# LayerNorm as two matrix products, wide matmuls as two column tiles, and a new plan of the order

## The chip, the cores and the metric

The program runs on one core of one Trainium2 chip. Five engines work side by side, each through its own queue in order: TensorE (PE; PEld is its loading of weights), VectorE (DVE), ScalarE (ACT), GpSimd (POOL) and SyncE (SP, which here only starts DMAs). The metric is the device time of one execution in microseconds, the median of several runs. All data is float32.

## The reference

Eight batches of 256 tokens of width 128 go through one cross attention with a gate, and then through a stack of six layers. Cut to what matters:

```python
x = x + tanh(g_xattn) * xattn(layernorm(x), ctx, ctx, ...)   # 16 heads of 8, 256 x 256 scores
y = layernorm(x)
for i in range(6):
    y = attn_layer(shift_tokens(y), Wqkv[i], q_scale[i], k_scale[i], Wo[i]) + y
    y = ffn_layer(shift_tokens(y), ln_g[i], ln_b[i], W1[i], b1[i], W2[i], b2[i]) + y
x = x + tanh(g_ffn) * y

def attn_layer(x, Wqkv, qs, ksc, Wo):          # 16 heads of 64, inner width 1024
    q, k, v = split(x @ Wqkv)
    q, k = rotary(l2norm(q) * qs), rotary(l2norm(k) * ksc)
    return local_attention(q, k, v) @ Wo       # windows of 32, each sees itself and the one before

def ffn_layer(x, g, bln, W1, b1, W2, b2):
    mu = x.mean(-1); var = ((x - mu) ** 2).mean(-1)
    xn = (x - mu) / sqrt(var + 1e-5) * g + bln
    a, gate = split(xn @ W1 + b1)              # 341 columns each
    return a * gelu(gate) @ W2 + b2
```

`shift_tokens` moves the second half of the features one token on. The part that is rewritten is `xn` in `ffn_layer`.

## The kernel before

The stream of a batch lives transposed in SBUF (`st[b]`, features on the partitions, 256 tokens along the row, the shifted half stored one column on), so a slice of it is the stationary operand of a projection. A piece of work for one layer and one batch is called a sequence here; there are 6 x 8 = 48, numbered k = 8 l + b. Each sequence has: eight projections of q and k, 128 tokens x 512 columns (`project`, L555); squares on ACT, rotation on DVE and its sum on POOL (`square` L563, `rotate` L571, `rotate_add` L586); norms and their inverses; POOL's multiplication by them (`normalize`, L609); transposes of q and k (`qk_transpose`, L619) and their evacuation by ACT (`qk_evacuate`, L627); v in four spans (`v_project`, L634), already written as two products of 64 columns of weights each, which go to the two halves of the partitions; scores in tiles of 64 rows and 32 columns (`scores`, L653); softmax over DVE, POOL and ACT (L664 to L691); transposes of the probabilities (`p_transpose`, L698); attention (`attend`, L730); the output projection in two halves of four accumulating products (`o_project`, L748); its addition to the stream (`o_add`, L539 and L540).

Then comes the feed-forward part. `f_transpose` (L761) turns the stream back to tokens on partitions, as two transposes into a PSUM tile px. `f_stats` takes mean and variance of each token on DVE (bn_stats L203, bn_aggr L204) and adds eps on ACT (L206). `f_rstd` raises to the power -0.5 on POOL (L210). `f_norm` subtracts and multiplies on DVE (L214), into xn in SBUF. `f_back` (L777) transposes xn again, and `f_affine` (L782) applies ln_g and ln_b on ACT, since features are then on the partitions. `f_up` (L797) makes three products for the gate and three for the values, the third of each with 85 columns of weights; `f_gelu` (L804), `f_gate` (L810), `f_down` (L821) and `f_add` follow.

The cross attention of the eight batches (`cross`, pieces whose names begin with x) fills the first 200 us nearly alone and runs beside the first sequences.

PSUM has three pools of two buffers: `ps_p` (one bank: projections, v, px, most of the cross part), `ps_s` (two banks: scores, transposes, attend, the up products) and `ps_m` (one bank: output projection, the transposed xn, two of the three value products, down). A piece that needs a buffer waits until the last reader of the buffer's old tile is done. Where DVE and ACT both read one PSUM tile, they read one after the other.

The order is written out by hand, in a table. `PLAN` gives each piece a time in slots, a sequence comes 5 slots after the one before it, and `CROSS_SHIFT` moves the cross part of each batch. All pieces are sorted by that time and emitted in that order, and each engine's queue holds its own in the same order:

```python
    def at(k, piece, fn, *args):
        time = PLAN[piece]
        pieces.append((k * SLOTS + time, len(pieces), fn, args))
```

So several sequences overlap. In the steady part, the order on PE over one sequence's time is: down (fdo) of k, proj31 of k+4, fba of k+1, proj30 of k+4, sc00 and sc01 of k+3, gate products (fga) of k+1, pt1 of k+2, proj00 of k+5, value products (fva) of k+1, vp3, sc10, sc11, vp1, vp2 of k+3, attend of k+2, proj01 and proj10 of k+5, wo0 of k+2, proj11, pqt3 and pqt0 of k+4, wo1, proj21, vp0, pqt2, pqt1, then ftr of k+2, proj20, pt0. Piece names: ftr, fst, frs, fno, fba, faf are f_transpose to f_affine in that order; vp and ve are v and its evacuation; sq, rot, radd, ss, nrm, qe, pqt are square to qk_transpose above; ma, mx, sub, ex, rs, div are the softmax's steps; pt and pe the transposes of probabilities and their evacuation; oe the evacuation of attend.

Weights of a layer are loaded by SP (`load_layer`, L475 to L500) into pools of two buffers, as soon as the last reader of the layer before the last is done.

Of the kernel before, what the change touches and what calls it, by code (L numbers as in the profile page):

```python
# [17 lines left out]
P = 128  # L18
# [12 lines left out]
FCH = [(0, 128), (128, 128), (256, FF - 256)]  # L31
EPS = 1e-5
# [5 lines left out]
    "clr": -73.7292947, "scb": -70.0069797, "ld0": -35.0162171, "ld1": -12.5813247,  # L38
    "tab": -7.6683787, "proj00": 2.0661479, "rot00": 2.4025502, "sq00": 2.5554862,
    "proj01": 3.2529434, "rot01": 3.3214336, "proj10": 3.5071971, "sq01": 3.6104712,  # L40
    "proj11": 3.6885065, "rot10": 3.7356190, "ss0": 3.7720268, "sq10": 3.7886707,
    "rot11": 3.8350533, "sq11": 3.8724995, "ss1": 3.9918618, "proj21": 4.0448072,
    "sq21": 4.3781883, "radd1": 4.3924623, "rot21": 4.4758648, "proj20": 4.8425580,
    "rot20": 5.5697729, "sq20": 5.5713267, "radd0": 5.9042720, "proj31": 6.2244486,
    "ss2": 6.2710763, "sq31": 6.3406736, "proj30": 6.4849253, "rot31": 6.5498143,
    "sq30": 6.6199673, "rot30": 6.7542538, "radd2": 6.9297661, "ss3": 7.1340866,
    "radd3": 7.2930704, "norms": 7.3485381, "ninv": 7.5627076, "nrm0": 7.5645782,
    "nrm3": 7.6018457, "nrm1": 8.2038284, "nrm2": 8.5657430, "pqt3": 8.6901898, "qe30": 8.8084477,
    "pqt0": 8.8257991, "vp0": 9.0734647, "qe31": 9.2292320, "pqt2": 9.2331941, "qe00": 9.3130114,
    "qe01": 9.3703632, "ve0": 9.3828160, "pqt1": 9.4414715, "qe21": 9.4630469, "qe10": 9.5406248,  # L50
    "qe20": 9.6465658, "qe11": 9.6687562, "sc00": 11.4869562, "sc01": 11.5828198,
    "ma0": 11.6476475, "mx0": 11.7176783, "vp3": 12.3428719, "sc10": 12.3554151,
    "ve3": 12.3847098, "sc11": 12.5047342, "sub0": 12.5264914, "ex0": 12.6176090,
    "vp1": 12.6566462, "vp2": 12.7494513, "ma1": 12.7820149, "ve2": 12.8886442, "rs0": 12.9868968,
    "ve1": 13.0757847, "mx1": 13.8703536, "div0": 14.6942876, "pt0": 14.9561638,
    "sub1": 15.0941710, "pe00": 15.1903495, "ex1": 15.7662187, "pe02": 15.9880113,
    "rs1": 16.3923268, "pe01": 16.6012453, "div1": 16.6632054, "pt1": 16.8318843,
    "pe12": 16.9812383, "pe10": 17.0871542, "pe11": 17.1065885, "at00": 17.8598296,
    "at01": 18.1229096, "at10": 18.2090149, "at11": 18.2185563, "oe0": 18.3505974,
    "wo0": 18.6691075, "oe1": 18.7595325, "wo1": 18.8332231, "oadd": 19.4264539,  # L60
    "ftr": 19.5952591, "fst": 19.8667684, "frs": 20.2036030, "fno": 20.9271736, "fba": 21.2395826,
    "faf": 21.7154140, "fga": 21.7794201, "fge": 21.8634391, "fva": 22.1636116, "fgt": 22.7262591,
    "fdo": 25.8686930, "fad": 27.9976703, "ldn": 28.7587942, "zt": 45.0036545, "zg": 45.1826346,
    "xld": -30.5179940, "xst": -28.7483611, "xrs": -28.2094646, "xno": -28.0294722,
    "xt": -25.8919641, "xte": -25.0068817, "xqk": -24.7151093, "xqe": -24.3960041,
    "xke0": -24.1822220, "xke1": -23.5897625, "xvp": -19.0992115, "xs1": -18.8011010,
    "xm11": -18.7695610, "xm12": -18.6001009, "xs0": -18.3761821, "xm10": -18.2076043,
    "xve": -18.1237548, "xm02": -18.0698775, "xm01": -18.0275400, "xs3": -17.5398786,
    "xm00": -17.3912921, "xm31": -17.3567125, "xm32": -17.2670533, "xm30": -16.6512482,
    "xs2": -16.4574966, "xm20": -15.6590289, "xm21": -15.4966539, "xb": -15.2142077,  # L70
    "xm22": -15.0420951, "xnt": -14.8243647, "xnc1": -14.7619952, "xp1": -14.7176089,
    "xnc2": -14.7060645, "xnc3": -14.7056110, "xe11": -14.6791462, "xe12": -14.6766048,
    "xe10": -14.4655074, "xnc0": -14.4380100, "xp0": -14.4183134, "xa1": -14.2088572,
    "xe02": -13.8510992, "xe01": -13.6172258, "xo1": -13.6088919, "xe00": -13.5855076,
    "xp3": -13.4284936, "xa0": -13.3512163, "xe31": -13.3313625, "xe32": -13.3038361,
    "xo0": -13.2546436, "xe30": -13.1766209, "xp2": -12.8009007, "xa3": -12.6439522,
    "xe22": -12.3901756, "xe21": -12.2805457, "xo3": -12.1606156, "xe20": -11.0882968,
    "xa2": -10.5369546, "xo2": -10.5038915, "xu1": -9.9444150, "xd1": -9.7892678,
    "xu0": -9.2798463, "xd0": -8.5766695, "xw": -7.7897065, "xc": -7.7481286, "xwo": -6.8890118,
    "xx": -6.8061458, "xst2": -6.6550961, "xr2": -6.5917848, "xn2": -6.4798693, "xt2": -5.6284344,  # L80
    "xsp": -5.5775580,
# [3 lines left out]
    -31.1859779, -28.1496673, -25.2253671, -22.2780463,  # L85
    -19.2671839, -16.3307478, -13.4009654, -10.5435620,
# [5 lines left out]
def tile_gated_block(ctx: ExitStack, tc: tile.TileContext, a: dict, out: bass.AP):  # L92
# [22 lines left out]
    def at(k, piece, fn, *args):  # L115
        time = PLAN[piece]
        pieces.append((k * SLOTS + time, len(pieces), fn, args))

# [12 lines left out]
    make_identity(nc, ident)  # L131
    half_neg = const.tile([P, 4], F32, name="half_neg")
# [86 lines left out]
    def cross(b):  # L219
# [32 lines left out]
        def x_project():  # L252
            pm = c_["pqk"] = ps_p.tile([P, 2, T], F32, tag="pj", name="pqk")
            for i in range(2):
                nc.tensor.matmul(pm[:, i, :], x_w[:, i, :], x_mid[:, i, :], start=True, stop=True)
# [15 lines left out]
        def x_values():  # L271
            pm = c_["pv"] = ps_p.tile([P, NT, D], F32, tag="pj", name="pv")
            for t in range(NT):
                nc.tensor.matmul(
                    pm[:, t, :], x_mid[:, 1, t * P : (t + 1) * P], x_w[:, 2, :],
                    start=True, stop=True,
                )
# [119 lines left out]
        def x_out():  # L397
            pm = c_["pout"] = ps_p.tile([P, NT, D], F32, tag="pj", name="pout")
            oT = c_.pop("oT")
            for t in range(NT):  # L400
                nc.tensor.matmul(pm[:, t, :], oT[:, t, :], x_w[:, 3, :], start=True, stop=True)
# [24 lines left out]
        kx = b + CROSS_SHIFT[b] / SLOTS  # L426
        for n, fn in (
# [8 lines left out]
            at(kx, n, fn)  # L436
        for part in range(2):
            at(kx, f"xke{part}", x_keys, part)
        for u in range(4):
            at(kx, f"xs{u}", x_scores, u)  # L440
            at(kx, f"xnc{u}", x_max_add, u)
            at(kx, f"xp{u}", x_scores_t, u)
            for x in range(3):
                at(kx, f"xm{u}{x}", x_maxima, u, x)
                at(kx, f"xe{u}{x}", x_exponentials, u, x)
            at(kx, f"xa{u}", x_attend, u)
            at(kx, f"xo{u}", x_attended, u)
        for t in range(NT):
            at(kx, f"xu{t}", x_turn, t)
            at(kx, f"xd{t}", x_divide, t)  # L450
# [20 lines left out]
    def load_layer(l):  # L471
# [14 lines left out]
        w["1"] = wpool.tile([P, 2 * FF], F32, tag="w1", name="w_1")  # L486
        nc.sync.dma_start(w["1"], a["L0_ffn_W1"][l])
# [56 lines left out]
    def sequence(k, l, b, weights):  # L544
# [4 lines left out]
        def project(c, half):  # L549
# [5 lines left out]
            nc.tensor.matmul(  # L555
# [188 lines left out]
        def o_project(half):  # L744
            first = "pwo" not in c_
            pm = once(c_, "pwo", ps_m, [P, T], "m")
            for c in range(4 * half, 4 * half + 4):
                nc.tensor.matmul(  # L748
# [8 lines left out]
        def f_transpose():  # L757
            px = ps_p.tile([P, NT, P], F32, tag="pj", name="px")
            c_["px"] = px
            for t in range(NT):  # L760
                nc.tensor.transpose(px[:, t, :], st[b][:, t * P : (t + 1) * P], ident)  # L761

        def f_stats():
            c_["mv"], c_["rstd"] = stats_of(c_["px"])
# [4 lines left out]
        def f_norm():  # L769
            c_["xn"] = wk.tile([P, NT, D], F32, tag="xn", name="xn", bufs=1)  # L770
            normalized(c_["xn"], c_.pop("px"), c_.pop("mv"), c_.pop("rstd"))

        def f_back():
            px = ps_m.tile([P, NT, P], F32, tag="m", name="pxt")
            c_["pxt"] = px
            for t in range(NT):
                nc.tensor.transpose(px[:, t, :], c_["xn"][:, t, :], ident)  # L777

        def f_affine():
# [3 lines left out]
                xnT, c_.pop("pxt").rearrange("p n t -> p (n t)"), AF.Identity,  # L783
# [3 lines left out]
        def f_up(s):  # L787
# [8 lines left out]
            for c, (o, m) in enumerate(FCH):  # L796
                nc.tensor.matmul(  # L797
                    dst[c][:m], w[:, s * FF + o : s * FF + o + m], c_["xnT"],
                    start=True, stop=True,
# [15 lines left out]
        def f_down():  # L815
            pm = ps_m.tile([P, T], F32, tag="m", name="pw2")
            c_["pw2"] = pm
            for c, (o, m) in enumerate(FCH):

                m += c == 2  # L820
                nc.tensor.matmul(  # L821
# [5 lines left out]

        for c in range(4):
            for half in range(2):
                at(k, f"proj{c}{half}", project, c, half)  # L830
                at(k, f"sq{c}{half}", square, c, half)
                at(k, f"rot{c}{half}", rotate, c, half)
                at(k, f"qe{c}{half}", qk_evacuate, c, half)
            at(k, f"pqt{c}", qk_transpose, c)
            at(k, f"ss{c}", squares_sum, c)
# [154 lines left out]
```

## Time and profile before

| | us |
|---|---|
| median of 3 runs | 1675.97 (1674.86 to 1676.92) |
| the profiled execution | 1670.12 |
| its span, first to last instruction | 1668.3 |
| PE busy in the span | 1601.3 |
| DVE, ACT, POOL busy | 1390.5, 1243.0, 1254.2 |
| start of the first projection of sequence 0 | 203.4 |
| first product of the output projection, sequences 10 and 11 | 593.4 and 622.3 |
| the same, sequences 46 and 47 | 1629.0 and 1645.4 |

A line of a timeline gives the start of a group of like instructions, the time from the first's start to the last's end, the engine, the source line, the operation, out <- in, the tile shape on the array (rows * columns), the shapes and the count. A float32 product shows as two records, a transpose as one. The ends of PE's records are modelled and overlap the next, so times on PE are taken between starts. Busy windows give, for each engine, the busy us in a stretch and the number of instructions; PEclk is the granted clock. The list of waits says who waited for whom, how long in total, and how often.

### The profile page before, as it was taken

What the parts mean: (1) busy time and instruction counts of PE and PEld (TensorE: products, weight loads), DVE (VectorE), ACT (ScalarE), POOL (GpSimd) and SP (SyncE); (2) the same over time, 40 slices, a digit from 0 to 9 for tenths busy, and PEclk for the clock granted to TensorE, in tenths of its full rate; (3) what the DMA queues carried; (4) which work ended last, traced back from release to release, by engine and by line L of the source; (5) the groups of instructions that cost most, each with busy time, mean ns of one, the idle gap of its engine ahead of it and who ended that gap; (6) DMA issues with size and microseconds to landing.
All of it is one profiled execution on the core that took longest, in us unless ns stands there. A gap on an engine that the chain in (4) does not pass through costs nothing.

```text
span 1668.3 us, 62716 instructions
## 1 busy us (share of the span) xinstructions
PE 1601.3 (96%) x28212; PEld 1011.2 (61%) x28212; DVE 1390.5 (83%) x1956; ACT 1243.0 (75%) x2084; POOL 1254.2 (75%) x714
## 2 busy tenths in 40 slices
PE   6989878999999999999999999999999999999996
PEld 3555534566666666666666666666666666666665
DVE  3455687899899989999899999899899999989964
ACT  3445447788787878888787888878787888878783
POOL 1112147988888898888888888888888988888871
PEclk8888899999999999999999999999999999999999
DMA  1300001000010000000000100000110000000000
GB/s 29 81 14 8 7 1 52 24 3 3 3 41 23 15 3 2 27 29 24 2 3 3 40 24 14 3 2 3 43 33 3 3 3 3 2 3 3 3 6 23
DMA packets 35208, 25.34 MB, mean 15 GB/s; under 512 B 16634, under 2 KB 31870, under 8 KB 34942
## 3 DMA queue, kind: packets, MB, share of 16 engines
q1 hardware_dynamic: 33646, 21.20, 4.4%
q8 instruction: 222, 3.64, 0.9%
q14 instruction: 44, 0.36, 0.1%
q10 hardware_dynamic: 1296, 0.14, 0.1%
HBM read 20.28 MB, written 1.05 MB: 13 GB/s over the span
## 4 chain that ended last, share of the span: by engine, by line
PE 86%; DVE 8%; ACT 3%; issue 1%; POOL 1%; DMA 1%; POOLq 0%; DVEq 0%; ACTq 0%
PE pj L555 21%; PE pv L634 11%; PE m L748 10%; PE s L653 8%; PE s L730 7%; PE pqt L619 6%; PE s L797 5%; PE pw L821 4%; DVE x_max L319 4%; PE ppt L698 4%; PE pa L797 2%; PE pssT L341 2%; PE pox L358 2%; ACT pr L351 1%; PE pssx L309 1%
## 5 line engine op out<-in xcount | busy, mean ns | idle before, releaser
L586 POOL TENSOR_TENSOR u<-ur 128x1024 f32<-128x1024 f32 x192 | 454.1, 2366 | 125.2 <-DVE ur L571 122.0
L555 PE MATMUL pj<-w_qkv,st 128*128 128x512 f32 x768 | 404.5, 619 | 9.0 <-ACT sq L563 2.8
L563 ACT ACTIVATE sq<-pj 128x512 f32<-128x512 f32 x384 | 229.5, 598 | 197.1 <-DVE ur L571 117.3
L609 POOL TENSOR_TENSOR u<-u,rn 128x1024 f32<-128x1024 f32 x192 | 359.2, 1900 | 3.6 <-DVE rn L602 3.6
L571 DVE TENSOR_TENSOR ur<-pj,rotk 128x1024 f32<-128x1024 f32 x192 | 234.7, 1222 | 63.9 <-PE pj L555 46.0
L571 DVE TENSOR_TENSOR ur<-pj,rotq 128x1024 f32<-128x1024 f32 x192 | 231.0, 1204 | 4.8 <-ACT sq L563 3.5
L580 DVE TENSOR_REDUCE squares<-sq 128x16 f32<-128x1024 f32 x192 | 232.1, 1209 | 0.9 <-ACT sq L563 0.7
L691 POOL TENSOR_TENSOR pr<-pr,rs 128x1024 f32<-128x1024 f32 x96 | 182.8, 1904 | 62.9 <-DVE rs L686 61.5
L210 POOL TENSOR_TENSOR rstd<-rstd,half_neg 128x2 f32<-128x2 f32 x64 | 45.0, 703 | 203.2 <-ACT rstd L206 187.2
L634 PE MATMUL pv<-w_qkv,st 128*64 128x512 f32 x768 | 197.1, 613 | 0.0
L748 PE MATMUL m<-oT,w_o 128*128 128x256 f32 x768 | 186.1, 386 | 0.0
L677 POOL TENSOR_TENSOR pr<-pr,top 128x1024 f32<-128x1024 f32 x96 | 182.7, 1903 | 1.1 <-DVE top L672 1.0
L653 PEld LDWEIGHTS s<-kT,qT 64*32 64x32 f32 x12288 | 127.2, 105 | 75.4 <-issue 40.3
L555 PEld LDWEIGHTS pj<-w_qkv,st 128*128 128x128 f32 x768 | 126.5, 190 | 72.6 <-issue 23.2
L748 PEld LDWEIGHTS m<-oT,w_o 128*128 128x128 f32 x768 | 141.9, 190 | 39.8 <-issue 21.5
L619 PEld LDWEIGHTS pqt<-ident,u 64*128 64x128 f32 x3072 | 102.9, 138 | 75.2 <-issue 39.7
L730 PEld LDWEIGHTS s<-prT,v 64*64 64x64 f32 x6144 | 122.0, 133 | 38.6 <-DVE hid L810 36.9
L653 PE MATMUL s<-kT,qT 64*32 64x64 f32 x12288 | 142.9, 225 | 0.0
L685 DVE TENSOR_REDUCE rs<-pr 128x16 f32<-128x1024 f32 x96 | 116.6, 1215 | 18.4 <-ACT pr L681 18.4
L319 DVE TENSOR_REDUCE x_max<-pssx 128x2 f32<-128x512 f32 (+1 forms) x96 | 77.5, 860 | 63.7 <-PE pssx L309 63.7
L730 PE MATMUL s<-prT,v 64*64 64x96 f32 (+1 forms) x6144 | 128.7, 238 | 0.0
L715 ACT ACTIVATE prT<-ppt,parity 128x256 f32<-128x256 f32 x192 | 121.4, 634 | 2.0 <-PE ppt L698 2.0
(112 smaller groups left out, 2674.9 us busy)
## 6 DMA issues: line engine op xcount, KB each, us to landing
w_qkv<-in_L_ffn_Wqkv SPq DMA_DIRECT2D x18, 512.0 KB
w_o<-in_L_ffn_Wo SPq DMA_DIRECT2D x24, 128.0 KB
w<-in_L_ffn_W SPq DMA_DIRECT2D x6, 341.0 KB
xin<-in_x SPq DMA_DIRECT2D x8, 128.0 KB
cin<-in_ctx SPq DMA_DIRECT2D x8, 128.0 KB
out<-res SPq DMA_DIRECT2D x8, 128.0 KB
w<-in_L_ffn_W SPq DMA_DIRECT2D x12, 64.0 KB
rotq<-in_c_cos_q SPq DMA_DIRECT2D x6, 64.0 KB
```

Of the source, the lines that this page charges most:

```text
L555: nc.tensor.matmul(pj, st[b][:, t * P : (t + 1) * P], w["qkv"][:, o : o + 512], start=True, stop=True,)
L563: nc.scalar.activation(sq[:, hs, :], c_["pj", c, half], AF.Square)
L571: nc.vector.tensor_tensor(ur[:, :, half * 512 : (half + 1) * 512].rearrange("p x (h d) -> p x h d", d=DH), pj.unsqueeze(1).to_broadcast([P ...
L580: nc.vector.tensor_reduce(squares[k % 2][:, t, i, :, 0], c_.pop(("sq", c)), AX.X, ALU.add)
L586: nc.gpsimd.tensor_tensor(u.rearrange("p h (two d) -> p h two d", two=2), ur[:, 0], ur[:, 1, :, ::-1, :], ALU.add,)
L609: nc.gpsimd.tensor_tensor(u, u, rn, ALU.mult)
L619: nc.tensor.transpose(pt[:, h, j, :], uf[rows, j * P : (j + 1) * P], ident[rows, rows])
L634: nc.tensor.matmul(pj[par * DH : (par + 1) * DH], st[b][:, e * KEYS : (e + 1) * KEYS], wv[:, par], start=True, stop=True,)
L653: nc.tensor.matmul(pss[n * WIN : (n + 1) * WIN, par, c, :], c_["qT"][rows, c, o : o + WIN], keys, start=True, stop=True,)
L691: nc.gpsimd.tensor_tensor(pr, pr, rs, ALU.mult)
L730: nc.tensor.matmul(po[half * DH : (half + 1) * DH, x, i, KEYS * e : q1], c_["v"][rows, e, c, :], prT[rows, e, c, : q1 - KEYS * e], start=n ...
L748: nc.tensor.matmul(pm, weights[l]["o"][:, c, :], oT[:, c, :], start=(first and c == 4 * half), stop=(not first and c == 4 * half + 3),)
```

## The change

It has three parts.

First, the feed-forward LayerNorm. With tokens as columns of the stationary operand, the product of the stream with the matrix `centre` (identity minus 1/128 everywhere) turns the stream and subtracts the mean at once. ACT squares the result with scale 128^-0.5 and sums along the row, which is the variance, adds eps, and copies the centred values to SBUF (`xc`). POOL raises to the power -0.5 as before. DVE makes `dg`, per block of tokens a diagonal matrix of the inverse deviations, and the product of `xc` with `dg` turns back and scales at once. Both products go to one tile `px` of one bank in `ps_m`; the ps_p buffer is no longer used here. The affine step is as before.

Second, `multiply`: all wide matmuls become two products of 64 columns of weights each, to the two halves of the partitions. It is used in project, o_project, f_up, f_down, the two LayerNorm products and the cross part's x_project, x_values and x_out. The third up product takes 128 columns in place of 85, so W1's tile is 43 columns wider, and one more DMA fills them. The transposes stay transposes, and v was already so.

Third, new numbers in `PLAN` and `CROSS_SHIFT`, and a small shift for each batch in the first and the last layer. In the steady part PE's order becomes: ftr of k+1, sc00 of k+3, pt0 of k+2, proj31 and proj30 of k+4, fdo of k, fba of k+1, sc01, fga, pt1, proj00 of k+5, fva, vp3, sc10, sc11, proj01, vp2, attend, vp1, proj10, wo0, proj11, pqt0, pqt3, wo1, proj21, vp0, pqt1, pqt2, proj20. On DVE: rot20, ss2, fno, rot31, rot30, ma0, ss3, mx0, rot00, fgt, ninv, ma1, mx1, rot01, rs0, fad, ss0, rot10, rot11, ss1, rs1, rot21, oadd. On ACT: sq20, fst, pe01, pe02, pe00, sq30, sq31, faf, fge, pe11, pe12, pe10, norms, ve3, sq00, ex0, ve2, oe0, sq01, oe1, ve1, sq11, sq10, ex1, qe01, qe00, qe31, qe30, sq21, ve0, qe10, qe11, qe20, qe21. On POOL: radd1, frs, div1, radd2, radd3, sub0, nrm3, nrm0, sub1, nrm2, nrm1, radd0, div0.

```diff
+FFP = P * len(FCH)
...
+    def multiply(out, lhsT, rhs, **kw):
+        for h in range(2):
+            o = slice(h * DH, (h + 1) * DH)
+            nc.tensor.matmul(out[o], lhsT[:, o], rhs, **kw)
...
+    centre = const.tile([P, P], F32, name="centre")
+    nc.gpsimd.tensor_scalar(centre, ident, -1.0 / D, None, ALU.add)
...
-        w["1"] = wpool.tile([P, 2 * FF], F32, tag="w1", name="w_1")
-        nc.sync.dma_start(w["1"], a["L0_ffn_W1"][l])
+        w["1"] = wpool.tile([P, FF + FFP], F32, tag="w1", name="w_1")
+        nc.sync.dma_start(w["1"][:, : 2 * FF], a["L0_ffn_W1"][l])
+        nc.sync.dma_start(w["1"][:, 2 * FF :], a["L0_ffn_W1"][l][:, : FFP - FF])
...
-            nc.tensor.matmul(
+            multiply(
                 pj, st[b][:, t * P : (t + 1) * P], w["qkv"][:, o : o + 512],
                 start=True, stop=True,
             )
...
-                nc.tensor.matmul(
+                multiply(
                     pm, weights[l]["o"][:, c, :], oT[:, c, :],
...
-        def f_transpose():
-            px = ps_p.tile([P, NT, P], F32, tag="pj", name="px")
-            c_["px"] = px
+        def f_center():
+            px = c_["px"] = ps_m.tile([P, 2, NT, D], F32, tag="m", name="px")
             for t in range(NT):
-                nc.tensor.transpose(px[:, t, :], st[b][:, t * P : (t + 1) * P], ident)
+                multiply(
+                    px[:, 0, t, :], st[b][:, t * P : (t + 1) * P], centre, start=True, stop=True
+                )
 
         def f_stats():
-            c_["mv"], c_["rstd"] = stats_of(c_["px"])
+            px = c_["px"][:, 0]
+            rstd = c_["rstd"] = small.tile([P, NT], F32, tag="rstd", name="rstd")
+            xc = c_["xc"] = wk.tile([P, NT, D], F32, tag="xn", name="xc", bufs=1)
+            for t in range(NT):
+                nc.scalar.activation(
+                    xc[:, t, :], px[:, t, :], AF.Square, scale=D**-0.5,
+                    accum_out=rstd[:, t : t + 1],
+                )
+            nc.scalar.activation(rstd, rstd, AF.Identity, bias=eps)
+            nc.scalar.copy(xc, px)
...
         def f_norm():
-            c_["xn"] = wk.tile([P, NT, D], F32, tag="xn", name="xn", bufs=1)
-            normalized(c_["xn"], c_.pop("px"), c_.pop("mv"), c_.pop("rstd"))
+            dg = c_["dg"] = wk.tile([P, NT, P], F32, tag="dg", name="dg", bufs=1)
+            nc.vector.tensor_tensor(
+                dg, ident.unsqueeze(1).to_broadcast([P, NT, P]),
+                c_.pop("rstd").unsqueeze(2).to_broadcast([P, NT, P]), ALU.mult,
+            )
 
         def f_back():
-            px = ps_m.tile([P, NT, P], F32, tag="m", name="pxt")
-            c_["pxt"] = px
+            xc, dg = c_.pop("xc"), c_.pop("dg")
             for t in range(NT):
-                nc.tensor.transpose(px[:, t, :], c_["xn"][:, t, :], ident)
+                multiply(c_["px"][:, 1, t, :], xc[:, t, :], dg[:, t, :], start=True, stop=True)
...
-                nc.tensor.matmul(
-                    dst[c][:m], w[:, s * FF + o : s * FF + o + m], c_["xnT"],
-                    start=True, stop=True,
+                multiply(
+                    dst[c], w[:, s * FF + o : s * FF + o + P], c_["xnT"], start=True, stop=True
                 )
...
-                nc.tensor.matmul(
+                multiply(
                     pm, weights[l]["2"][:m, c, :], hid[:m, c, :], start=(c == 0), stop=(c == 2)
                 )
```

## The prediction

> **What bounds the kernel now.** I read the page first (parts 1, 2 and 4), then the busy times of ten whole sequences in the middle, then TensorE's timeline over one sequence, then the waits.
>
> ```profile
> PE 1601.3 (96%) x28212; PEld 1011.2 (61%) x28212; DVE 1390.5 (83%) x1956; ACT 1243.0 (75%) x2084; POOL 1254.2 (75%) x714
> ...
> PE   6989878999999999999999999999999999999996
> ...
> PE 86%; DVE 8%; ACT 3%; issue 1%; POOL 1%; DMA 1%; POOLq 0%; DVEq 0%; ACTq 0%
> ```
>
> ```profile
> 800.00:1089.60 289.60, 289.60 (x5504) 185.06 (x5500) 262.47 (x351) 235.72 (x391) 252.94 (x134) 1.00 0.04 13
> ```
>
> The window holds ten sequences: PE is busy in all of its 289.6 us, DVE in 262.5, ACT in 235.7, POOL in 252.9, at clock 1.00. So one sequence costs 28.96 us, and its price is the sum of what stands on PE. A busy PE can still hide gaps, so the starts on its timeline have to be read:
>
> ```profile
> 806.88 1.56 PE L821 MATMUL pw<-hid,w 128*128 128x256 f32 x6
> 808.42 1.12 PE L555 MATMUL pj<-w_qkv,st 128*128 128x512 f32 x2
> 809.38 0.38 PE L777 MATMUL pxt<-ident,xn 128*128 128x128 f32 x2
> 809.60 1.02 PE L555 MATMUL pj<-w_qkv,st 128*128 128x512 f32 x2
> 810.55 1.49 PE L653 MATMUL s<-kT,qT 64*32 64x64 f32 x128
> 811.97 1.56 PE L797 MATMUL s<-xnT,w 128*128 128x256 f32 x6
> 813.46 0.71 PE L698 MATMUL ppt<-ident,pr 64*128 64x64 f32 x16
> 814.10 1.13 PE L555 MATMUL pj<-w_qkv,st 128*128 128x512 f32 x2
> ...
> 816.45 1.08 PE L634 MATMUL pv<-w_qkv,st 128*64 128x512 f32 x4
> 817.46 1.49 PE L653 MATMUL s<-kT,qT 64*32 64x64 f32 x128
> 818.88 1.94 PE L634 MATMUL pv<-w_qkv,st 128*64 128x512 f32 x8
> 820.74 2.67 PE L730 MATMUL s<-prT,v 64*64 64x96 f32 x128
> 823.35 1.98 PE L555 MATMUL pj<-w_qkv,st 128*128 128x512 f32 x4
> 825.17 1.89 PE L748 MATMUL m<-oT,w_o 128*128 128x256 f32 x8
> 826.89 1.02 PE L555 MATMUL pj<-w_qkv,st 128*128 128x512 f32 x2
> ```
>
> ```profile
> PEld pj L555 <- DVE xn L214: 17.9, 45, 1.4
> ```
>
> Prices come from differences of starts. A product shows as two records (two passes), a transpose as one. L748 follows L555 in the same tile shape: 826.89-825.17 = 1.72 for 8 records, so 0.215 a pass at 256 columns, no gap. L777 to L555: 0.22 for two, 0.11 at 128 columns. L555 x4: 1.82 for four passes of 0.43 plus 0.10, which is paid on entering 128*128 from another shape (the second pass waits for its weights). L797 x6: 1.49 = 6x0.215 + 0.10 entry + 0.10 on leaving. The 128*64 products of v are two column tiles side by side: x4 takes 1.01, x8 1.86 (820.74-818.88), so four more records (one more full 128x512 result) cost 0.85 to 0.86, the same 0.43 a pass; what is left, 0.15, is 0.05 entry and 0.10 leaving. So a change of shape costs 0.10, and entering wide work 0.10 more as 128*128 and 0.05 as 128*64. Last, 808.42-806.88 = 1.54 is 0.15 over 6x0.215 + 0.10 entry, and the projection behind it pays its 0.10 entry again without any change of shape: that is the wait on DVE's xn, 0.24 us, in 45 of 48 sequences.
>
> **The change, part by part** (us per sequence on PE, from the order in which each plan puts the pieces).
> 1. LayerNorm. Out go 4 transposes of 0.11; in come 4 products of 128 columns, each two passes, as column tiles: 8x0.11. Together **+0.44**. No row has a 128-column pass in the 128*64 shape: below, 0.11 as the transposes; above, 0.14, their 0.11 plus the 0.03 that half an entry costs, would make it +0.68. I take 0.11, since the pairs at 512 columns pay nothing over the full shape.
> 2. Entries. Before, five entries of 0.10 (down, gate, first projection, the projection after attend, second half of the output projection), one of 0.06 (the px transposes) and three of 0.05 (v) make 0.71. After, all wide work is 128*64 and has seven runs: 0.35. **-0.36.**
> 3. Changes of shape. In the old plan one sequence has 16, with v and the rest switching into each other three times; in the new one 15: **-0.10**. The first score piece is split in two runs, which pays the score shape's small entry once more: **+0.03**.
> 4. The wait on xn. px was one of two ps_p buffers and held proj31 up until DVE had normalised. Now px lies in ps_m and is released by faf: **-0.24**.
> 5. The wide products themselves (8 projections, 8 output, 6 up, 3 down) become 25 more instructions, passes unchanged: 0, at worst 0.01 for each of 50 passes, +0.5; the v pairs show 0.
>
> Sum -0.23. Here the Trainium skill speaks against the change: its page "TensorEngine Tiling (Array Packing)", Performance Considerations (Instruction Overhead), gives every matmul some 60 cycles of overhead and warns against tiling a dimension without need. Worked out from that page with the skill's 2.4 GHz, the 29 more matmuls of a sequence would be estimated at +0.73 us, some +32 us over 44 sequences, and the kernel slower at about 1700. The x8 row above shows no such overhead at 512 columns, so the sum goes by the row; no row shows it at 256 or 128.
>
> What stands beside PE. DVE loses 4 statistics and aggregates (0.93) and two normalisations (0.73), and gets one 128x256 product (0.35 to 0.48: half the 1024-element pitch to the L810 row at 0.476). ACT loses nothing and gains two squares with a sum, and a copy of 0.37 (L366's 0.378). POOL is unchanged. By the window, DVE goes from 26.2 to 25.0, ACT from 23.6 to about 24.7, under PE's 28.7. So no engine takes over; what counts is single waits. I walked the queues of the new order over one sequence with these rows:
>
> ```profile
> 804.57 0.59 ACT L627 COPY kT<-pqt 128x512 f32<-128x512 f32 x1
> 805.07 0.59 ACT L627 COPY qT<-pqt 128x512 f32<-128x512 f32 x1
> 805.55 0.59 ACT L627 COPY kT<-pqt 128x512 f32<-128x512 f32 x1
> ```
>
> From the start of the pqt1/pqt2 run: 0.73 until the first copy, four copies at 0.48, square 0.60, rot20 1.23, squares' sum 1.13 (DVE's back-to-back pitch), the diagonal 0.35, rot31 1.23, square 0.6, affine 0.57, hand-overs 0.25 between: 8.4 us, then fga may start. PE has 8.36 us of its own work from there to fga. Likewise from proj21's end to ftr PE has 3.0, and square, rot21, oadd and hand-overs need 2.97. Both just fit. Everything else has 0.15 or more (sc11 behind the gate) and most has over 1 (POOL's inverse norms and both divides). An error of 0.1 in either becomes a wait, so I keep **+0.03**: -0.20, or 28.76 a sequence.
>
> The squares with a sum have no row: below, 0.27 (L366 scaled to 128 columns by the slope to L563's 598 for 512), above, 0.60, L563's whole 512 columns. I take 0.35, near the low end, as they have a quarter of its columns. The queue behind them on ACT (three prT copies, two squares, the affine) has 0.4 to spare, so up to 0.5 each costs nothing.
>
> Ends. The ramp keeps its order: the cross chains are serial over DVE maxima and ACT exponentials, some 27.3 us for each batch (107.36 to 134.69 on the chain), and proj00 of the first sequence stands behind the same cross piece. x_project, x_values and x_out change shape now beside transposes, at most two more changes a batch (+0.2), and xqk moves into a stretch where PE waits for maxima. I put 0 for both, ±4 in all. In the tail, sub1 and its exponentials of the last sequence come earlier, so pt1, which waited on POOL there, can start: -1 (0 to -2). The last LayerNorm chain is the old 3.1 us (px 1650.07, pxt 1653.15) against 2.8 with the rows above and a product 0.2 longer: 0. The constant `centre` and the extra load of W1's tail cost 0: POOL is busy 18.8 of the first 100 us, and layer 2's loads go out at 473 while its first projection comes near 669.
>
> Sum: 44 sequences at full pitch x -0.20 = -8.8, tail -1: about -10. The profiled execution took 1670.12 (span 1668.3); the median of the runs is 5.85 above it, which I carry along: 1668.3 - 9.8 = 1658.5 span, 1660.3 profiled, **1666** as a median.
>
> **The rivals.**
> A, forecast: PE stays the bound, at 28.7 to 28.85 a sequence: 1661 to 1671. For it: the x8 row, the full window. 0.50.
> B: the two tight places (ftr behind oadd, fga behind faf) take back what entries save. At 0.2 more a sequence the time is 1675. For it: the old plan also left a wait of 0.24. Against: DVE gets 1.2 us free. 0.15.
> C, the other side: ACT becomes late behind the squares with a sum. Each 0.1 over 0.5 apiece delays sq30, sq31 and the affine by 0.2, and PE waits at fga. It decides from 0.6 each (wait of 0.2 eats the gain); at 0.7, +0.2 a sequence, 1684. For it: no row of them; against: 128 columns only. 0.10.
> D: column passes at 256 and 128 columns cost more than the full shape. From 0.004 a pass over the 58 passes the gain is gone; at 0.01, +0.38 a sequence, 1692. Against: the v pairs. 0.08.
> E: no wait is left, the extra 0.05 of the projection in front of pt0 (1.00 from 805.24 to 806.24, against 0.96 for the one at 826.89) goes as well, and the cross chains gain 4: 1655 to 1660. 0.17.
>
> About 0.2% (3.4 us) is what a measurement of this kernel can tell from no change. Faster: A and E, 0.67; same: B, 0.15; slower: C and D, 0.18. The range leaves out D and the far ends of C and E: 1655 to 1682; A's own is 1661 to 1671.
>
> **What would show it.** The pitch between sequences falls from 28.96 to about 28.76; wide runs show 128*64 with 0.05 entry; the wait on xn is gone from the list; a pair of 128-column records takes 0.11. Against me: waits of PE on faf or oadd in most sequences (B, or C if the squares exceed 0.5), pairs over 0.22 at 256 columns (D), or a first projection much off 203 us.

## The result, and the profile after

The changed kernel takes 1703.13 us (median of 4 runs, 1700.79 to 1707.25) against 1675.76 (1674.86 to 1676.92): a ratio of 1.0169, 95% interval 1.0149 to 1.0189. It is slower by 27 us, where 1666 with a range of 1655 to 1682 was predicted. Parts 1 and 4 of the page of the changed kernel (busy time of each engine, and the chain that ended last by engine):

```profile
PE 1605.3 (94%) x31284; PEld 942.3 (55%) x31284; DVE 1390.3 (82%) x1716; ACT 1268.8 (75%) x2324; POOL 1267.2 (75%) x715
...
PE 63%; DVE 19%; ACT 14%; issue 2%; DMA 0%; POOL 0%; POOLq 0%; DVEq 0%; ACTq 0%
```

PE's share of the chain falls from 86% to 63%, and DVE's rises from 8% to 19%, although DVE has 240 instructions fewer. Busy times of the stretch shown for the kernel before (start:end and length, then PE, PEld, DVE, ACT, POOL, the clock, DMA share and GB/s):

```profile
800.00:1089.60 289.60, 282.78 (x5852) 166.19 (x5848) 255.59 (x291) 234.21 (x432) 248.76 (x130) 1.00 0.04 13
```

PE was busy in all of this stretch before; now it idles in 6.8 of 289.6 us, at the same granted clock of 1.00. From Gelu to Gelu of successive sequences, the usual step is 29.67 us against 28.95; 28.76 was predicted. The list of waits (waiting engine, tile and line, who released it: total us, times, longest) names the place, the gate's product `fga` behind the affine:

```profile
PE s L132 <- ACT xnT L812: 31.3, 46, 0.7
```

It comes in 46 of 48 sequences, where nothing like it stood before. The timelines of PE, ACT, DVE and POOL in the same sequence (start, length, engine, line, operation) lead back from there:

```profile
813.83 1.47 PE L132 MATMUL pw<-hid,w 128*64 128x256 f32 x12
815.26 0.66 PE L132 MATMUL px<-dg,xc 128*64 128x128 f32 x8
815.85 0.86 PE L671 MATMUL s<-kT,qT 64*32 64x64 f32 x64
817.39 1.52 PE L132 MATMUL s<-xnT,w 128*64 128x256 f32 x12 [0.68 <-ACT xnT L812]
```

```profile
811.20 0.32 ACT L787 ACTIVATE xc<-px 128x128 f32<-128x128 f32 x1
811.36 0.24 ACT L787 ACTIVATION_READ_ACCUMULATOR xc<-px 128x1 f32 x1
811.45 0.32 ACT L787 ACTIVATE xc<-px 128x128 f32<-128x128 f32 x1
...
811.89 0.30 ACT L791 ACTIVATE rstd<-rstd,eps 128x2 f32<-128x2 f32 x1
...
816.28 0.60 ACT L581 ACTIVATE sq<-pj 128x512 f32<-128x512 f32 x1 [1.64 <-DVE ur L589]
816.78 0.56 ACT L812 ACTIVATE xnT<-px,ln_b,ln_g 128x256 f32<-128x256 f32 x1
```

```profile
812.52 1.21 DVE L598 TENSOR_REDUCE squares<-sq 128x16 f32<-128x1024 f32 x1
813.65 1.47 DVE L799 TENSOR_TENSOR dg<-ident,rstd 128x256 f32<-128x256 f32 x1
815.04 2.34 DVE L589 TENSOR_TENSOR ur<-pj,rotq 128x1024 f32<-128x1024 f32 x2
```

```profile
812.26 0.70 POOL L227 TENSOR_TENSOR rstd<-rstd,half_neg 128x2 f32<-128x2 f32 x1 [1.51 <-ACT rstd L791]
812.93 1.91 POOL L709 TENSOR_TENSOR pr<-pr,rs 128x1024 f32<-128x1024 f32 x1
814.79 2.55 POOL L604 TENSOR_TENSOR u<-ur 128x1024 f32<-128x1024 f32 x1
```

The affine stands on ACT behind a square that waited 1.64 us for DVE's rotation, and the rotation stood behind the diagonal `dg`, which took 1.47 us. The prediction had given it 0.35. The three records also show when it ended: at 815.12, which is 0.28 us after POOL's division had ended at 814.84. This holds whatever the start: over the first 47 diagonals of this run the end lies 0.277 to 0.282 us behind the end of an instruction of POOL. The first one took 4.39 us, since two of POOL's instructions passed it by (305.19 to 307.09 and 307.05 to 309.39):

```profile
305.28 4.39 DVE L799 TENSOR_TENSOR dg<-ident,rstd 128x256 f32<-128x256 f32 x1
```

Only the last diagonal, at 1684.09, found POOL idle; it took 0.42 us. So the time is no property of the 256 elements. No list of waits names it: the profile shows it as a long, busy DVE instruction.

### The profile page after: what moved, and what is told of

Same layout as the page of the kernel before. It is cut to its first block, busy times and chain, and to the rows that moved or that the text cites. A ratio compares the mean times of both kernels' runs of the same rounds, so it can differ in the third digit from the quotient of the medians.

```text
span 1700.1 us, 68801 instructions
## 1 busy us (share of the span) xinstructions
PE 1605.3 (94%) x31284; PEld 942.3 (55%) x31284; DVE 1390.3 (82%) x1716; ACT 1268.8 (75%) x2324; POOL 1267.2 (75%) x715
## 4 chain that ended last, share of the span: by engine, by line
PE 63%; DVE 19%; ACT 14%; issue 2%; DMA 0%; POOL 0%; POOLq 0%; DVEq 0%; ACTq 0%
PE pj L132 13%; PE pv L652 10%; PE m L132 10%; PE s L748 7%; DVE ur L589 7%; PE s L132 5%; PE pqt L637 5%; PE s L671 4%; DVE dg L799 4%; ACT sq L581 3%; DVE squares L598 3%; DVE x_max L336 3%; ACT qT L645 3%; ACT kT L645 3%; PE pa L132 2%; PE pox L375 2%
## 5 line engine op out<-in xcount | busy, mean ns | idle before, releaser
L604 POOL TENSOR_TENSOR u<-ur 128x1024 f32<-128x1024 f32 x192 | 464.8, 2421 | 28.8 <-DVE ur L589 19.5
L132 PE MATMUL pj<-w_qkv,st 128*64 128x512 f32 x1536 | 396.9, 608 | 4.5 <-ACT sq L581 1.9
L132 PE MATMUL m<-oT,w_o 128*64 128x256 f32 x1536 | 184.4, 382 | 0.0
L709 POOL TENSOR_TENSOR pr<-pr,rs 128x1024 f32<-128x1024 f32 x96 | 182.9, 1905 | 0.0
L671 PEld LDWEIGHTS s<-kT,qT 64*32 64x32 f32 x12288 | 130.9, 105 | 55.8 <-DVE hid L839 32.3
L671 PE MATMUL s<-kT,qT 64*32 64x64 f32 x12288 | 154.6, 226 | 0.7 <-ACT prT L725 0.4
L132 PEld LDWEIGHTS m<-oT,w_o 128*64 128x64 f32 x1536 | 106.2, 137 | 70.7 <-issue 24.7
L132 PEld LDWEIGHTS pj<-w_qkv,st 128*64 128x64 f32 x1536 | 92.6, 136 | 94.8 <-issue 27.6
L132 PE MATMUL s<-xnT,w 128*64 128x256 f32 x768 | 104.4, 394 | 33.0 <-ACT xnT L812 31.3
L659 ACT COPY v<-pv 128x512 f32<-128x512 f32 x192 | 112.3, 585 | 17.1 <-PE pv L652 17.0
```

What stands on the lines that cost most here:

```text
L132: nc.tensor.matmul(out[o], lhsT[:, o], rhs, **kw)
L604: nc.gpsimd.tensor_tensor(u.rearrange("p h (two d) -> p h two d", two=2), ur[:, 0], ur[:, 1, :, ::-1, :], ALU.add,)
L671: nc.tensor.matmul(pss[n * WIN : (n + 1) * WIN, par, c, :], c_["qT"][rows, c, o : o + WIN], keys, start=True, stop=True,)
L709: nc.gpsimd.tensor_tensor(pr, pr, rs, ALU.mult)
```

## The experiments

**Where the time goes: theories.** L: a DVE instruction that reads two tensors from SBUF (both `ident` and `rstd` lie there) stands until the POOL instruction beside it has ended. B: an operand that is repeated along the row makes DVE slow. S: the squares with their accumulator reads make ACT late (the prediction's rival C). Four kernels differ from the changed one in the diagonal alone, the fourth also in the operands of the product that uses it.

On ScalarE:

```diff
-            nc.vector.tensor_tensor(dg, ident..., rstd..., ALU.mult)
+            for t in range(NT):
+                nc.scalar.activation(dg[:, t, :], ident, AF.Copy, scale=rstd[:, t : t + 1])
```

> The diagonal is made by ScalarE, as two copies of the identity with the inverse deviation as scale; all else as in the changed kernel (1703.1 us, 29.67 us a sequence, of which PE waits 0.68 on the affine and about 0.16 on the diagonal). Theory L (VectorE's product, the only one that reads two operands from SBUF, stands until the GpSimd instruction beside it has ended): VectorE gets 1.47 us free, the two waits go, two ScalarE copies of 0.3 to 0.4 cost PE nothing; a sequence takes 28.8 to 28.95 and the kernel 1660 to 1668. Theory S (the squares with their accumulator reads, 0.57 each, make ScalarE late): ScalarE gets still more work, the wait on the affine stays at 0.6 or more, the time at 1695 or above. Theory B (an operand repeated along the row costs VectorE 6 ns an element) expects the same as L here.

On GpSimd:

```diff
-            nc.vector.tensor_tensor(
+            nc.gpsimd.tensor_tensor(
                 dg, ident.unsqueeze(1).to_broadcast([P, NT, P]),
```

> The same one product with both repeated operands, on GpSimd, behind its inverse deviation and before its division by the sums. Theory L: with both readers on one engine there is nothing to wait for; 256 elements take about 0.5 us by GpSimd's 1.9 us for 1024, VectorE is free, 28.8 to 28.95 us a sequence, 1660 to 1668. Theory S: the wait on the affine stays, 1695 or above. Theory B says nothing of GpSimd.

On VectorE as two products by one value a row:

```diff
+            for t in range(NT):
+                nc.vector.tensor_scalar(dg[:, t, :], ident, rstd[:, t : t + 1], None, ALU.mult)
```

> Still on VectorE, but as two products of the identity by one value a row, so that only one operand is a tensor in SBUF and none is repeated. Theory B: 0.3 to 0.4 us each, no wait, 1662 to 1670. Theory L as narrow as it can be (two SBUF tensors are needed): the same 1662 to 1670. Theory L in a wider form (a product from SBUF to SBUF waits for GpSimd too): the first ends about 0.3 us behind the division, and the second may have to wait for the whole next GpSimd instruction (2.4 us), so that PE waits up to 2 us more in each sequence: 1700 to 1790.

On VectorE, from PSUM. What comes out is the normalised block instead of a diagonal, and the second product turns it:

```diff
             nc.vector.tensor_tensor(
-                dg, ident.unsqueeze(1).to_broadcast([P, NT, P]),
+                dg, c_["px"][:, 0],
                 rstd.unsqueeze(2).to_broadcast([P, NT, P]), ALU.mult,
...
-                multiply(c_["px"][:, 1, t, :], xc[:, t, :], dg[:, t, :], start=True, stop=True)
+                multiply(c_["px"][:, 1, t, :], dg[:, t, :], ident, start=True, stop=True)
```

> The same VectorE instruction in shape, with the inverse deviation still repeated along the row, but its first operand is the centred px in PSUM in place of the identity in SBUF; what comes out is the normalised row block, and the second product turns it with the identity as its other operand. Theory L: one SBUF operand, no wait for GpSimd: 0.35 to 0.5 us, 28.8 to 28.95 a sequence, 1660 to 1668. Theory B: the repeated operand is still there, 1.5 us, 1700 to 1705. Theory S: 1695 or above.

Measured, against the kernel before (the usual step, and the sum of 44 steps from the first Gelu to the 45th; what lies ahead of the first and behind the 45th). Each ratio is to runs of the kernel before made beside that kernel, so it is not quite the quotient of two medians of the table:

| kernel | median us | ratio, 95% interval | step | 44 steps | ahead | behind |
|---|---|---|---|---|---|---|
| before | 1675.76 | | 28.95 | 1274.4 | 321.1 | 72.8 |
| changed | 1703.13 | 1.0169 (1.0149 to 1.0189) | 29.67 | 1308.3 | 314.1 | 77.7 |
| dg_on_scalar_engine | 1661.05 | 0.9909 (0.9887 to 0.9931) | 28.76 | 1271.8 | 313.3 | 74.4 |
| dg_on_gpsimd | 1655.28 | 0.9881 (0.9858 to 0.9905) | 28.76 | 1270.3 | 312.4 | 76.2 |
| dg_two_scalar_products | 1837.08 | 1.0950 (1.0923 to 1.0976) | 31.9 to 34.5 | 1445.4 | 316.9 | 76.7 |
| normalised_from_psum | 1657.14 | 0.9885 (0.9869 to 0.9902) | 28.76 | 1269.9 | 309.2 | 72.8 |

The groups of the instruction in the changed kernel, then in these four, in the order of the table (busy us, mean ns of one, and the idle time before it with its releaser):

```profile
L799 DVE TENSOR_TENSOR dg<-ident,rstd 128x256 f32<-128x256 f32 x48 | 73.5, 1532 | 8.8 <-POOL rstd L227 8.8
```

```profile
L801 ACT ACTIVATE dg<-ident,rstd 128x128 f32<-128x128 f32 x96 | 33.5, 404 | 3.4 <-POOL rstd L227 3.4
```

```profile
L799 POOL TENSOR_TENSOR dg<-ident,rstd 128x256 f32<-128x256 f32 x48 | 29.5, 614 | 3.8
```

```profile
L801 DVE TENSOR_SCALAR dg<-ident,rstd 128x128 f32<-128x128 f32 x96 | 165.8, 1766 | 8.8 <-POOL rstd L227 8.8
```

```profile
L799 DVE TENSOR_TENSOR dg<-px,rstd 128x256 f32<-128x256 f32 x48 | 19.9, 415 | 8.8 <-POOL rstd L227 8.8
```

The same DVE instruction with its first operand in PSUM takes 0.415 us in place of 1.53, with `rstd` still repeated along the row and POOL's division running beside it in nearly all sequences: B falls. S falls with the ScalarE version, in which ACT does more and PE's wait is gone. L stands, and in its wider form: a product by one value a row, with one tensor in SBUF, waits for POOL too. DVE and POOL of that kernel, from their timelines:

```profile
798.99 3.56 DVE L801 TENSOR_SCALAR dg<-ident,rstd 128x128 f32<-128x128 f32 x2
802.47 2.34 DVE L589 TENSOR_TENSOR ur<-pj,rotq 128x1024 f32<-128x1024 f32 x2
```

```profile
798.26 1.90 POOL L709 TENSOR_TENSOR pr<-pr,rs 128x1024 f32<-128x1024 f32 x1
800.12 2.34 POOL L604 TENSOR_TENSOR u<-ur 128x1024 f32<-128x1024 f32 x1
```

The first product ends 0.08 us behind POOL's L709, the second 0.08 us behind L604: each stood for one whole instruction of POOL or the rest of it. Most of the first took 1.26 us, most of the second 2.38. The five of the 96 that met an idle POOL took 0.27 to 0.29. That cost more than I had expected at worst (1837 us against 1790).

In the three kernels that avoid the wait, PE's usual step is 28.76 us. Its timeline in normalised_from_psum, the same four groups as above:

```profile
824.59 1.47 PE L132 MATMUL pw<-hid,w 128*64 128x256 f32 x12
825.89 0.61 PE L132 MATMUL px<-ident,dg 128*64 128x128 f32 x8
826.43 0.86 PE L671 MATMUL s<-kT,qT 64*32 64x64 f32 x64
827.21 1.52 PE L132 MATMUL s<-xnT,w 128*64 128x256 f32 x12
```

Between starts: down 1.30 against 1.43, px 0.54 against 0.59, scores 0.78 against 1.54. These three differences make 0.94, which covers the 0.91 of 29.67 less 28.76.

**Does the wait follow POOL's instruction?** In the order's list one number is changed, so that another POOL instruction stands beside the diagonal:

```diff
-    "div1": 16.0753193,
+    "div1": 16.9850000,
```

> The changed kernel with its diagonal untouched on VectorE; one piece of the order is moved: GpSimd's second division by the sums (div1, the L709 instruction that runs beside every diagonal) stands behind the rotation sum radd2. GpSimd then has nothing to do when the diagonal comes, since radd2 waits for a product that VectorE makes after the diagonal. Theory L: the diagonal takes 0.28 to 0.45 us in place of 1.47 in nearly all sequences, and the waits of PE on the diagonal and the affine go; the division ends 3 to 4 us later, so PE waits on it 1 to 1.6 us ahead of the second transposes of the probabilities, which makes 29.8 to 30.4 a sequence, 1705 to 1735 in all. Theory B (the cost is the instruction's own): still 1.47, 30.5 or more, 1740 and up.

The piece landed behind pt1, so the second block's probabilities are used undivided here, and PE doesn't wait for the division. My expectation was wrong on two more counts: radd2's product is made ahead of the diagonal, so POOL was not idle in most sequences, and its L604, the longer instruction, took the division's place. One run: 1727.55 us, usual step 30.15. DVE and POOL:

```profile
825.16 1.93 DVE L799 TENSOR_TENSOR dg<-ident,rstd 128x256 f32<-128x256 f32 x1
```

```profile
823.77 0.70 POOL L227 TENSOR_TENSOR rstd<-rstd,half_neg 128x2 f32<-128x2 f32 x1 [1.41 <-ACT rstd L791]
824.44 2.36 POOL L604 TENSOR_TENSOR u<-ur 128x1024 f32<-128x1024 f32 x1
```

It is a clearer test than the one I meant. The untouched DVE instruction now takes 1.93 us in place of 1.47, its end again 0.28 behind POOL's; POOL's instruction is 2.36 long in place of 1.90. The step grew by 0.48 us, the same 0.46 within 0.02.

The idle POOL that I had expected came too, in 10 of the 48 sequences, most of them the first and the last: there no instruction of POOL stands beside the diagonal, and the same instruction takes 0.41 to 0.43 us. In the other 38, L604 runs beside it, and it takes 1.93 to 2.59. One of the ten, on DVE, POOL and PE:

```profile
1522.82 0.41 DVE L799 TENSOR_TENSOR dg<-ident,rstd 128x256 f32<-128x256 f32 x1
```

```profile
1521.43 0.70 POOL L227 TENSOR_TENSOR rstd<-rstd,half_neg 128x2 f32<-128x2 f32 x1 [0.86 <-ACT rstd L791]
1527.86 1.91 POOL L709 TENSOR_TENSOR pr<-pr,rs 128x1024 f32<-128x1024 f32 x1 [5.72 <-PE ppt L716]
```

```profile
1523.00 1.47 PE L132 MATMUL pw<-hid,w 128*64 128x256 f32 x12
1524.30 0.61 PE L132 MATMUL px<-dg,xc 128*64 128x128 f32 x8
1524.83 0.86 PE L671 MATMUL s<-kT,qT 64*32 64x64 f32 x64
1525.62 1.52 PE L132 MATMUL s<-xnT,w 128*64 128x256 f32 x12
```

PE's starts lie 1.30, 0.53 and 0.79 apart, as in normalised_from_psum: with the instruction unchanged and POOL idle, the wait is gone. This leaves nothing of theory B.

**What each part of the change is worth.** The kernel before with the tiles alone (`multiply` at the wide products and the wider W1; old order and old LayerNorm):

```diff
-            nc.tensor.matmul(pj, ...)
+            multiply(pj, ...)
```

> The kernel before with nothing but the column tiles: old order, old LayerNorm with its transposes, 28.96 us a sequence. By the prediction's prices the tiles merge the values with the other wide products (two changes of shape less, -0.2, and two entries) and halve five entries (-0.25 to -0.30), but the two pairs of full-shape transposes, which stood beside products of their own shape, now change shape in front or behind (+0.4): 28.7 to 28.85, 1664 to 1671. If column passes cost more than full ones (rival D, 0.004 us or more a pass), 29.0 or more, 1678 and up.

The kernel normalised_from_psum with `multiply` undone:

```diff
     def multiply(out, lhsT, rhs, **kw):
-        for h in range(2):
-            o = slice(h * DH, (h + 1) * DH)
-            nc.tensor.matmul(out[o], lhsT[:, o], rhs, **kw)
+        nc.tensor.matmul(out, lhsT, rhs, **kw)
```

> The kernel of normalised_from_psum (28.76 us a sequence, 1657 us) with the wide products in full shape again, one matmul each; the values stay column tiles as they always were. By the prices: seven entries of 0.10 in place of 0.05 (+0.35), and four changes between values and the rest which the new order does not avoid (+0.4, and 0.2 to 0.3 for their entries): 29.6 to 29.9 a sequence, 1693 to 1708, slower than before. If the tiles save no more than the entries, 29.1, about 1672.

The same kernel with tiles, but `PLAN` and `CROSS_SHIFT` of before, and no shifts of single layers:

```diff
-FIRST_SHIFT = [-0.1834213, ...]
-LAST_SHIFT = [-0.0554613, ...]
+FIRST_SHIFT = LAST_SHIFT = [0.0] * 8
```

> The operations of normalised_from_psum in the order of the kernel before. By the prices: 28.96 less the wait of 0.24, plus 0.44 for the LayerNorm products, less 0.6 for entries and merged shapes: 28.56 a sequence if no new wait comes, 1647 to 1655. The old order was made for another LayerNorm, so waits of PE on xnT or oadd up to 0.4 may come: up to 29.0, 1670. If the new order is what gives most, 29.0 or more.

The changed kernel with the LayerNorm of before, in the new buffers:

```diff
-                multiply(px[:, 0, t, :], st[b][:, t * P : (t + 1) * P], centre, ...)
+                nc.tensor.transpose(px[:, 0, t, :], st[b][:, t * P : (t + 1) * P], ident)
...
+            c_["mv"], c_["rstd"] = stats_of(c_["px"][:, 0])
...
+            normalized(xn, c_["px"][:, 0], c_.pop("mv"), c_.pop("rstd"))
...
+                nc.tensor.transpose(c_["px"][:, 1, t, :], c_["xn"][:, t, :], ident)
```

> The changed kernel with the old LayerNorm (transposes, statistics and normalisation on VectorE), its two results in the buffers of the new one; wide products stay column tiles. VectorE reads PSUM only, so nothing waits for GpSimd. By the prices PE has 0.44 less for products and 0.3 more for two more changes of shape: 28.6 without waits. VectorE carries 1.66 us in place of 0.42, 1.2 more ahead of rot31, which is what the diagonal's 1.47 did: so a wait on the affine of 0.4 to 0.8 comes back, 29.1 to 29.5 a sequence, 1675 to 1692. If the order alone were the gain, 28.6 to 28.8, 1650 to 1660.

| kernel | median us | ratio, 95% interval | step | 44 steps | ahead | behind |
|---|---|---|---|---|---|---|
| tiles_alone | 1671.32 | 0.9980 (0.9960 to 0.9999) | 28.75 | 1271.3 | 326.5 | 72.4 |
| full_width_in_new_order | 1697.07 | 1.0150 (1.0129 to 1.0172) | 29.67 | 1307.9 | 313.9 | 73.9 |
| old_order_new_operations | 1673.22 | 0.9991 (0.9976 to 1.0007) | 28.80 | 1274.4 | 324.4 | 73.8 |
| old_layernorm_new_order | 1668.47 | 0.9965 (0.9951 to 0.9978) | 29.00 | 1280.1 | 313.3 | 72.7 |

The prices of PE's entries and changes of shape forecast the steps: 28.7 to 28.85 for the tiles alone (28.75), 29.6 to 29.9 without tiles (29.67). The new order needs the tiles: they are worth 0.91 us a sequence there (29.67 less 28.76), and 0.20 in the old one. The old order with the new operations was to be 28.56 without waits; it has a wait of some 0.18 on the affine (1.59 from scores to gate against 1.41), the other 0.06 of 28.80 less 28.56 is not traced, and it ends no faster than before. Its time and that of the tiles alone lie a little above what I expected, which the columns beside the step explain: their first Gelu comes 3 to 5 us later than before, and single steps are longer (below).

With the old LayerNorm in the new order the wait on the affine is back, shorter than expected; PE's timeline:

```profile
804.85 0.86 PE L671 MATMUL s<-kT,qT 64*32 64x64 f32 x64
806.05 1.52 PE L132 MATMUL s<-xnT,w 128*64 128x256 f32 x12 [0.34 <-ACT xnT L797]
```

The step of 29.00 less this 0.34 is 28.66, near the 28.6 forecast for PE's own work; DVE's 1.66 us of statistics and normalisation cost only 0.34 of wait where the diagonal's 1.47 cost 0.68.

**A version without the dead copy.** From normalised_from_psum, ACT's copy to `xc` is left out, since nothing reads it:

```diff
-            nc.scalar.copy(xc, px)
```

> The kernel of normalised_from_psum (1657 us, 28.76 a sequence, its PE without a wait) without ScalarE's copy of the centred block to SBUF (0.35 us a sequence), which nothing reads any more. PE bounds it, so ScalarE's time is worth nothing: 28.76 a sequence, 1653 to 1660. If ScalarE were late anywhere (theory S), up to 0.35 a sequence, 1640 to 1650.

1655.95 us, ratio 0.9883 (0.9850 to 0.9917), step 28.76: as forecast, ACT's 0.35 us is worth nothing. With dg_on_gpsimd and normalised_from_psum it is faster than both kernels by 1.2% and 2.8%; these three cannot be told apart.

## Why the prediction was wrong

The step that failed is one term: "the diagonal 0.35" in the walk from pqt1/pqt2 to `fga`. It measured 1.53 on average and 1.47 in nearly all sequences. The upper bound of 0.48 is the L810 row, one of whose two tensors lies in PSUM; the lower bound does not come out of its row, since half of a 1024-element pitch of 1.13 to 1.23 is about 0.6, and 256 elements are a quarter. The trace of before has no DVE instruction in its steady part that reads two tensors from SBUF. It has sums that read one (L580): these took 1.20 to 1.22 us in all 192 cases, 190 of them beside a busy POOL. So the nearest row was near in size and far in kind, and neither bound held beside POOL; alone, the instruction does take the 0.42 that lies between them. What the prediction called tight did the rest: "An error of 0.1 in either becomes a wait" was said of `fga`, and an error of 1.1 became a wait of 0.76 there and of 0.18 ahead of and in the second product. 0.91 a sequence over 44 makes 40 us between 28.76 and 29.67.

The walk also has a slip in its sum. Its terms come to 8.36, and to 8.61 with the hand-overs, not to 8.4; added up rightly, it would have forecast a wait of 0.25 even with a diagonal of 0.35. Measured from the start of the pqt1/pqt2 run to `fga`, the stretch takes 8.41 in normalised_from_psum (818.80 to 827.21, no wait of PE) and 9.35 in the changed kernel (808.04 to 817.39). So 8.4 was near the truth, but by luck, since it is not the sum of its terms.

The changed kernel's tail is 5 us longer than that of normalised_from_psum; the diagonals there take up to 2.11, but the two other versions without the wait have 74.4 and 76.2, so not all of it need be the diagonal's. The sign that was named against the forecast, PE waiting on the affine in most sequences, is the one that came.

The rule that would have said so is in the Trainium skill, in its page "SBUF — State Buffer", section "Who interferes with whom": a VectorE instruction with two inputs in SBUF contends with a GpSimd instruction that reads SBUF, whoever comes first holds the ports for its whole length, and `tensor_scalar`, the product by a scalar, can contend as well, in the modes in which it uses both ports. The runs agree on each count, though no run shows the ports or the mode: 1.47 and 1.93 us beside POOL, 0.41 to 0.43 beside none, 0.415 from PSUM, 1.77 in the mean for a product by a scalar against 0.27 to 0.29 beside an idle POOL. POOL waits too where it comes second: its L604 behind the diagonal takes 2.55 us, and 2.34 in the kernel of two products. Why POOL's next instruction passed the waiting diagonal by in the first sequence and not in the later ones is open.

Point by point:
- The sum on PE, 28.76, was right to 0.01 as soon as the diagonal no longer waited. So were its terms: a 128-column pass as a column tile costs 0.11 (px 0.54 to 0.55 for four pairs with 0.10 on leaving), and the wait on xn is gone from the list. Rival D is out: a pair of 512-column tiles takes 0.43 and sixteen records of 256 take 1.73 (799.76 to 800.62 to 802.35 in the changed kernel).
- The rule weighed there from the Trainium skill's page "TensorEngine Tiling (Array Packing)", Performance Considerations (Instruction Overhead), some 60 cycles of overhead for each matmul, is not seen as an addition to each: the tiles alone, 25 more matmuls a sequence, took the step from 28.95 to 28.75. The same section says that a product of one column takes as long as one of 60; read as such a floor, it would add nothing here, where the narrowest product has 64 columns. Its warning is against a tiling factor from a dimension that is already small; the prediction put that too broadly.
- The squares were priced well: 0.69 us for two between starts (811.20 to 811.89), each 0.32 with an accumulator read of 0.25 that overlaps its neighbours; 0.35 each was taken, 0.5 was the threshold. Rival C named the place, `fga`, but neither the cause nor the size: its 1684 stood for squares of 0.7 each.
- Rival B's other tight place, `ftr` behind oadd, did not make PE wait (1.9 us in all): the 30.2 us of that wait in the list are weight loads that wait beside PE's own work, and they stand unchanged in the kernels with a step of 28.76.
- 0 was wrong for the ramp. The first projection comes at 201 us as before (203), but the first Gelu at 309 to 317 in all kernels of the new order, against 321 to 327 in the three of the old. Of the 16.4 us by which normalised_from_psum's span is shorter than that of before (1651.9 against 1668.3), 11.9 are in that stretch and 4.5 in the steps. PE's busy share from 200 to 300 us rises from 85 to 89%, and the granted clock there from 0.94 to 0.98. Which of the new times does it wasn't tried, nor whether the clock is a cause or a consequence. So that kernel's 1657 lies below the forecast of 1666 mainly by this stretch, which the prediction put at 0.
- The tail was put at -1; without the diagonal's wait it is 0 (72.8 in both).

## What to carry to other kernels

A cost taken from a row of the trace needs the same memories for its operands, not only the same engine and size. Before a VectorE instruction that reads two tensors from SBUF, or multiplies one from SBUF to SBUF by a value a row, is put beside a busy GpSimd, look at what GpSimd runs at that moment, and add the rest of that instruction to the price; reading one operand from PSUM, or moving the work to ScalarE or GpSimd, avoids it. A long busy instruction with no wait listed can itself be a wait: compare the ends of its records with the ends of another engine's.

## What the runs showed of the hardware that I had not expected

Single steps come out longer in all the kernels built here. Before, none of the 44 is over 29.05; in normalised_from_psum five are between 29.01 and 29.95, in all 4.5 us above 44 x 28.76, about half of what the shorter step saves. With full-width products in the new order it is 2.4 us above 44 x 29.67, with the tiles alone in the old order 6.3 above 44 x 28.75. One of them, on PE's timeline:

```profile
924.92 0.64 PE L652 MATMUL pv<-w_qkv,st 128*64 128x512 f32 x1
925.98 0.65 PE L652 MATMUL pv<-w_qkv,st 128*64 128x512 f32 x2 [0.42 <-issue]
926.46 0.59 PE L132 MATMUL pj<-w_qkv,st 128*64 128x512 f32 x1
926.46 0.59 PE L652 MATMUL pv<-w_qkv,st 128*64 128x512 f32 x1
```

The first of a pair ran alone, the next instruction came 1.06 us later without waiting for anyone, and from there the two halves ran one product apart (a projection beside a value product). Why the instruction came late is open: the changed kernel fetches 245 packets of instructions where the kernel before fetched 222, but the full-width one, with 223, has longer steps too.
